# Gate logits by linearity in a pre-LN attention and feed-forward kernel

## Chip, cores and metric

The kernel runs on one core of one Trainium2 chip. The metric is the device time of one execution in microseconds. Lower is better. Times are told as the median of several runs; the profile is one further execution.

## What is computed

Two batches of 2048 tokens with 1024 features pass through two layers, all in float32. The first is attention with a head size of 256, the second a feed-forward layer with a router. Both take a normalised input and add their output to the residual.

```
x = x + attn(layernorm(x), Wqkv, bqkv, Wo, bo)      # q, k, v of width 256; softmax; @ Wo + bo
x = x + ffn(layernorm(x), ...)

def ffn(hidden, gate_w, up_w, down_w, fc1_w, fc2_w, expert_w, ln_gamma, ln_beta):
    logits = einsum('bsh,he->bse', hidden, gate_w)          # 8 experts
    routing_weights, _ = top_k(logits, 2)
    h = relu(einsum('bsh,hi->bsi', hidden, up_w)) ** 2      # 2048 wide
    shared_out = einsum('bsi,ih->bsh', h, down_w)
    x_latent = einsum('bsh,hl->bsl', hidden, fc1_w)         # 512 wide
    expert_out = einsum('bsl,lm->bsm', x_latent, expert_w)
    moe_out = expert_out * sum(routing_weights, axis=-1)
    routed_out = einsum('bsl,lh->bsh', moe_out, fc2_w)
    return layernorm(shared_out + routed_out, ln_gamma, ln_beta)
```

Of the router only one number per token is used: the sum of its two largest gate logits. It scales the latent part.

## The kernel before

Products keep nearly float32 accuracy by splitting each operand into a high part and a low part (`split`: ScalarE writes the high part, VectorE or GpSimd subtracts it for the low part). `Pass3` (L131) then issues three products for each pair of operands: high with high, low with high, high with low. Tokens are handled in eight blocks of 512 (`W`), each of four tiles of 128.

The kernel has four stages in order of time.

1. *Start* (`begin`). Expert weights are folded into fc2, the first block is normalised, and the QKV weights are split. The weights of V are stored with high and low parts side by side, 512 columns per chunk.
2. *QKV* (`a_block`, `qkv_block`). For each of eight blocks, V is computed in four tiles (`v_tile`, L447), then q and k in four chunks. Beside it, after each of the eight parts, the function `after(j)` normalises the next block, transposes it through DRAM and splits it. `NormBlock`, `Moments` and `Stats` hold the statistics. This stage, except for its last block, is written in the order in which it is issued (`manual_schedule`).
3. *Attention*. A loop over n computes the scores of block n, the values of block n - 1, and then `finish` and `project` (L726) for it: the product with Wo in two halves of 512 columns, multiplied by the inverse of the softmax sum and added to the residual, which already holds bo. The result goes to DRAM as `x1`. A scheduler orders the instructions here. The bank pools for TensorE's results are `psa` (four banks), `psb` and `psc` (two each).
4. *Feed-forward*. Four passes over two blocks each. An up stage and a down stage use a seven-product scheme on 2x2 block matrices (pieces `p1` to `p7`). Its order is written by hand. `next_piece` brings one weight piece: SP's queue loads it, ScalarE (L939) and VectorE (L946) split it. `Norm` normalises the blocks that come next, `Out` finishes the blocks that came before.

The gate sits in the up stages. `gate_part` (L995) multiplies one half of the normalised input with the gate weights: four products with 32 columns (8 high, 8 low, 16 zero) and four with 8 columns, all streaming 512 tokens. It is called four times in each up stage, for pieces p1, p2, p4 and p3; a copy on ScalarE (L1310) and three operations on VectorE (L1313, L1316, L1318) put the halves together. `Gate.largest` (L1013 to L1025) transposes the logits in 32x32 blocks, adds the high and low parts, takes the eight largest of each token (`max`, sixteen times), adds the first two, and transposes again. `send` (L1030) writes the result to DRAM and `spread` (L1034) reads it back to all partitions as `rwb`. Both are on POOL's queue. In the products that use them, the latent columns are multiplied by `rwb`.

`half` tiles (512 columns, four buffers), `row` tiles (1024 columns, nine) and `unit` tiles (2048 columns, fourteen) share the on-chip memory. Queues issue in order: SP's carries weights, residual rows and stores of `x1`; POOL's carries normalised tiles, kept weight pieces, bo, beta and the output.

Of the kernel before, what the change touches and what calls it, by code (L numbers as in the profile page):

```python
# [25 lines left out]
def kernel(  # L26
# [65 lines left out]

    def bank(pool, name):
        return pool.tile([P, W], FP, tag="b", name=name)
# [11 lines left out]
    bv_sb = half("bv")[:, :D]  # L106

    gate = const.tile([P, NCC, SQ], FR, name="gate")
    nc.vector.memset(gate.bitcast(FP), 0.0)
# [6 lines left out]
    fc2e = dram.tile([LAT, C], FP, name="fc2e")  # L116

# [54 lines left out]
    def ln_stats(parts, st=None):  # L172


        if st is None:
            st = small.tile([P, C // W, 6], FP, tag="st", name="st")
        for h, part in enumerate(parts):
            if part is not None:
                nc.vector.bn_stats(st[:, h, :], part)  # L179
        mv = small.tile([P, 2], FP, tag="mv", name="mv")  # L180
        nc.vector.bn_aggr(mv, st.rearrange("p a b -> p (a b)"))
        sd = small.tile([P, 1], FP, tag="sd", name="sd")
        nc.scalar.activation(sd, mv[:, 1:2], AF.Sqrt, bias=eps)
        return mv[:, 0:1], sd
# [11 lines left out]
    def norm_row(r, q=nc.gpsimd):  # L196
        return norm_write(r, row_stats(r), q)

    def row_stats(r):
        return ln_stats([r[:, ts(h, W)] for h in range(C // W)])  # L200

    def normalise(r, stats):
        mean, sd = stats
        nc.vector.tensor_scalar(r, r, mean, inverse(sd), ALU.subtract, ALU.mult)

    def norm_write(r, stats, q=nc.gpsimd):


        normalise(r, stats)
        return transpose_write(r, q)  # L210
# [44 lines left out]
    class Moments:  # L255


        def __init__(self, v, kind):
            self.v, self.kind = v, kind
# [5 lines left out]
        def new(self, a):  # L265
            return small.tile([P, 1], FP, tag=self.kind + a, name=a)
# [15 lines left out]
        def normalise(self):  # L282

            rs, nb = self.inverse(), self.new("nb")
            nc.vector.tensor_tensor(nb, self.nm, rs, ALU.mult)
            nc.scalar.activation(self.v, self.v, AF.Identity, scale=rs, bias=nb)  # L286

    class Stats(Moments):


        def __init__(self, v):
            self.v, self.kind = v, "n"
            mean, self.sd = row_stats(v)
# [6 lines left out]
    class NormBlock:  # L300
# [5 lines left out]
        def step(self, t):  # L306
            rows, m = self.rows, self.m
            if t == 0:
                m += [Moments(rows[0], "n"), Stats(rows[1])]
                m[0].second()  # L310
                m[0].normalise()
                m.append(Moments(rows[2], "n"))
# [4 lines left out]
            if t < NB:  # L317
                self.d.append(transpose_write(rows[t]))
                if t == 0:
                    m.append(Stats(rows[3]))  # L320
# [106 lines left out]
    def qkv_block(n, wqkv, xT, parts, after):  # L427
# [9 lines left out]
        def v_tile(t):  # L437
# [4 lines left out]
            for c in range(NCC):  # L442
                xh, xl = x_chunk(xT, c, ts(t, P))
                w = wqkv[2][c // 4].rearrange("p (c n) -> p c n", n=2 * D)[:, c % 4]
                ops = [(pm, xh, w), (pm[:, :D], xl, w[:, :D])]
                for i, (o, x_, w_) in enumerate(ops[:: -1 if c % 2 else 1]):
                    nc.tensor.matmul(  # L447
                        o,
# [3 lines left out]
                        stop=c == NCC - 1 and i == 1,  # L452
# [4 lines left out]
            nc.vector.tensor_tensor(vt, pm[:, D : 2 * D], vt, ALU.add)  # L457
# [29 lines left out]

    order = list(range(BPB, NBLK)) + list(range(BPB))
    def begin(wqkv, xT):
# [18 lines left out]
        nc.gpsimd.dma_start(out=bv_sb, in_=bqkv[2 * D : 3 * D].partition_broadcast(P))  # L508

# [52 lines left out]
        stats = [row_stats(first[0])]  # L562
        for t in range(NB):
            if t + 1 < NB:
                stats.append(row_stats(first[t + 1]))
            normalise(first[t], stats[t])
            if t == 1:
                r = [folded(0, accs)]
        wqkv[2] = []

        def beside(t, lc):
# [5 lines left out]
            if t in (1, 2):  # L577
                u = unit(f"w2_{t}")
                uv = u.rearrange("p (c n) -> p c n", n=2 * D)
                wv = ws[2][1].rearrange("p (c n) -> p c n", n=D)[:, ts(t - 1, NCC // 2)]  # L580
                split(wv, uv[:, :, 0:D], uv[:, :, D : 2 * D], nc.gpsimd)
                wqkv[2].append(u)
# [4 lines left out]
        return NormBlock(rows), r  # L587
# [120 lines left out]
    def project(n):  # L708
        s = st.pop(n)
        o = hl(s["oT"])  # L710
        for t in range(NB):
# [5 lines left out]
            for h in range(C // W):  # L717

                pm = bank(psa if n + 1 < NBLK else psc, "pw")
                acc = Pass3(pm, NDC)  # L720
                for dc in range(NDC):
                    acc.add(
                        tuple(o[:, i, ds(dc * W + t * P, P)] for i in range(2)),
                        piece(wo, dc, C, ts(h, W)),
                    )
                nc.vector.scalar_tensor_tensor(  # L726
                    r[:, ts(h, W)], pm, s["ri"][:, t : t + 1], r[:, ts(h, W)], ALU.mult, ALU.add
                )
            nc.sync.dma_start(out=x1[n][ts(t, P), :], in_=r)
# [4 lines left out]
    def a_block(i, norm, xT, x3):  # L734
# [5 lines left out]
        def after(j):  # L740
            if i + 1 == NBLK:
                if j == 0:
                    x3()
                elif j == 2 * NB - 1:
# [22 lines left out]
        qkv_block(order[i], wqkv, xT, V + QK, after)  # L767
        if nxt:
            return (after_next or [None])[0], nxt[0], lambda: split_tile(norm.x[3], 3, nxt[0])

    wqkv, xT = {}, new_xT("a")
    with tc.manual_schedule():
        steps = list(range(len(STEPS)))
        norm, fold = begin(wqkv, xT)
        x3 = lambda: None
        for i in range(NBLK - 1):
            norm, xT, x3 = a_block(i, norm, xT, x3)
# [9 lines left out]
    with tc.issue_after(fetched[0].ins):  # L787
        q_rows = [load_row(q_d[i], nc.gpsimd) for i in range(2)]
    a_block(NBLK - 1, None, xT, x3)

    with tc.issue_after(fetched[0].ins):
        wo_f = [load_row(Wo[ts(dc, P), :], nc.gpsimd) for dc in range(NDC)]

    g_f = half("g_f")[:, : NCC * NE].rearrange("p (c e) -> p c e", c=NCC)
    nc.gpsimd.dma_start(out=g_f, in_=gate_w.rearrange("(c p) e -> p c e", p=P))
    xts = []
    for n in range(1, NBLK + 1):
# [4 lines left out]
        for k in range(NKC + lag):  # L802
# [21 lines left out]
            elif k == 5 and n in range(3, 3 + NB):  # L824
                xts[n - 3] = norm_row(xts[n - 3], nc.sync)
# [8 lines left out]
            if n == 1 and k == NKC // 2:  # L834
                wo = unit("wo_h"), unit("wo_l")
                for dc in range(NDC):
                    split(wo_f[dc], *(v[:, ts(dc, C)] for v in wo))
                split(g_f, gate[:, :, 0:NE], gate[:, :, NE : 2 * NE])
# [151 lines left out]
    def gate_part(X, half):  # L990
        pg = bank(psc, "pg")
        for i in range(2):
            for c in range(4):
                m = NE if i else SQ
                nc.tensor.matmul(  # L995
                    pg[:m, :],
                    lhsT=gate[:, half * 4 + c, 0:m],
                    rhs=piece(X, c, W, slice(0, W))[i],
                    start=(i == 0 and c == 0),
                    stop=(i == 1 and c == 3),  # L1000
                )
        return pg[:SQ, :]

    class Gate:


        def __init__(self, gs):
            self.gs = gs

        def largest(self):  # L1010
            nb = W // SQ
            g, o = half("gtt")[:SQ, :], half("gtop")[:SQ, :]
            nc.vector.transpose(g, self.gs)  # L1013
            lg, m8 = (
                o[:, ds(i * nb * NE, nb * NE)].rearrange("p (b e) -> p b e", e=NE)
                for i in range(2)
            )
            gv = g.rearrange("p (b f) -> p b f", f=SQ)[:, :, 0 : 2 * NE]
            nc.vector.tensor_reduce(
                lg, gv.rearrange("p b (j e) -> p b e j", e=NE), AX.X, ALU.add  # L1020
            )
            for b in range(nb):
                nc.vector.max(m8[:, b, :], lg[:, b, :])
            nc.vector.tensor_tensor(o[:, 0:nb], m8[:, :, 0], m8[:, :, 1], ALU.add)
            nc.vector.transpose(o[:, ds(SQ, SQ)], o[:, 0:SQ])  # L1025
            self.rw = o[0:nb, ds(SQ, SQ)]

        def send(self):
            self.d = dram.tile([W // SQ, SQ], FP, tag="rw", name="rw_d", bufs=2)
            nc.gpsimd.dma_start(out=self.d, in_=self.rw)  # L1030

        def spread(self):
            rwb = half("rwb")
            nc.gpsimd.dma_start(  # L1034
                out=rwb, in_=self.d.rearrange("b i -> (b i)").partition_broadcast(P)
            )
            return rwb

    class Norm:
# [8 lines left out]
        def step(self, halves=(0, 1)):  # L1048
# [4 lines left out]
            if 0 in halves:  # L1053
# [4 lines left out]
                if norm in range(NB):  # L1058
                    self.m[norm].normalise()
            if 1 in halves:  # L1060
# [6 lines left out]
                if fetch in range(NB):  # L1067
                    self.x[fetch] = fetch_tile(self.d[fetch])
                self.i += 1
# [88 lines left out]
    with tc.manual_schedule():  # L1158
        for b in range(NBB):
# [72 lines left out]
            gm, gl = (6, 2) if b else (11, 1)  # L1232
            for m, (p, i) in enumerate(UPS[b]):
# [74 lines left out]
                if (p, i) == ("p1", 0 if b else 4):  # L1308
                    ga = half("ga")[:SQ, :]
                    nc.scalar.copy(ga, gate_part(X["p1"], 0))  # L1310
                elif (p, i) == ("p2", 0):
                    gs = half("gs")[:SQ, :]
                    add(gs, ga, gate_part(X["p2"], 1), ALU.add)  # L1313
                    gt = Gate(gs)
                elif (p, i) == ("p4", 1):
                    add(ga, ga, gate_part(X["p4"], 1), ALU.add)  # L1316
                elif (p, i) == ("p3", 6):
                    add(ga, ga, gate_part(X["p7"], 0), ALU.subtract)  # L1318
                    gt = Gate(ga)
                if m == gm or (p, i) == ("p3", 7):  # L1320
                    gt.largest()
                elif m == gm + gl or (p, i) == ("p3", 9):
                    gt.send()
# [150 lines left out]
```

## Time and profile before

| What | us |
|---|---|
| timed runs: median | 2317.57 |
| timed runs: lowest, highest | 2316.97, 2319.35 |
| profiled execution: its own time | 2321.8 |
| profiled execution: span on the core | 2320.0 |
| start, until V of the first block | 0 to 35 |
| eight QKV blocks | 35 to 302 |
| attention | 302 to 757 |
| four up stages | 757 to 952, 1143 to 1343, 1533 to 1731, 1922 to 2120 |
| four down stages | the stretches behind them, to 2320 |

The profile lists instructions by engine: PE is TensorE's products, PEld its weight loads, DVE is VectorE, ACT ScalarE, POOL GpSimd, SP the queue of SyncE. A line such as `pw<-wo_h,o` names what is written and what is read, and L131 is a line of the kernel. A product's length in the profile includes its way through the array, so the spacing of starts tells its cost in a row of products, not its length. The stage limits in the table are read from the first product of each kind in the timeline.

### The profile page before, as it was taken

How to read it: one execution, taken by the hardware profiler on the slowest of the kernel's cores; microseconds unless marked ns; L12 is line 12 of the kernel's file. 1: busy time of each engine (PE TensorE's matmuls, PEld its weight loads, DVE VectorE, ACT ScalarE, POOL GpSimd, SP SyncE). 2: the span in 40 equal slices, each digit the busy share in tenths (PEclk: the TensorE clock that was granted, in tenths of full speed). 3: DMA queues.
4: the chain of work that ended last, by engine and by line, in shares of the span. 5: the costliest groups of instructions: out<-in, count | busy, mean ns of one | idle time of the engine just before them, and what ended most of it. 6: DMA issues, size and time to landing. Idle time of an engine off the chain costs nothing.

```text
span 2320.0 us, 28848 instructions
## 1 busy us (share of the span) xinstructions
PE 2302.3 (99%) x10332; PEld 1894.8 (82%) x10332; DVE 1569.6 (68%) x2463; ACT 1187.1 (51%) x1955; POOL 284.3 (12%) x429
## 2 busy tenths in 40 slices
PE   9999999999999999999999999999999999999998
PEld 7888788888888788888878888888888888888886
DVE  6666569888878576797665577764456677435667
ACT  6555455555544633766562474664055566214245
POOL 3222211011000111110111111110000011000000
PEclk9999999999999999999999999999999999999999
DMA  7877749799986677786787688687568569556674
GB/s 255 296 279 278 245 140 263 229 303 295 228 192 188 216 225 227 258 286 199 216 240 246 228 306 313 186 250 218 192 217 273 192 210 274 188 186 198 204 223 150
DMA packets 236304, 540.28 MB, mean 233 GB/s; under 512 B 18513, under 2 KB 105041, under 8 KB 234113
## 3 DMA queue, kind: packets, MB, share of 16 engines
q1 hardware_dynamic: 170448, 301.25, 39.5%
q0 software_dynamic: 65712, 237.19, 35.0%
q8 instruction: 82, 1.34, 0.2%
q14 instruction: 62, 0.50, 0.1%
HBM read 411.47 MB, written 177.75 MB: 254 GB/s over the span
## 4 chain that ended last, share of the span: by engine, by line
PE 87%; DVE 6%; DMA 2%; issue 2%; ACT 2%; POOL 0%; SPq 0%; DVEq 0%; ACTq 0%; POOLq 0%
PE pd L131 33%; PE pu L131 31%; PE ps L131 8%; PE po L131 8%; PE pw L131 4%; DVE xblk L214 2%; PE pg L995 1%; DMA xt_d<-xblk 1%; DVE xla L144 1%; PE pq L131 1%; PE pf L131 1%; DVE st L179 1%; DMA raw<-in_L_ffn_up_w_dram 0%; ACT junk L274 0%; DVE v L457 0%
## 5 line engine op out<-in xcount | busy, mean ns | idle before, releaser
L131 PE MATMUL pd<-w,sp 128*128 128x512 f32 x3336 | 757.7, 390 | 0.1
L131 PEld LDWEIGHTS pd<-w,sp 128*128 128x128 f32 x3336 | 626.4, 188 | 130.3 <-DVE sp L1207 0.8
L131 PE MATMUL pu<-xh,w 128*128 128x512 f32 x2240 | 691.5, 390 | 1.9 <-DVE w L946 1.8
L131 PEld LDWEIGHTS pu<-xh,w 128*128 128x128 f32 x2240 | 420.7, 188 | 91.6 <-DVE w L946 2.7
L131 PE MATMUL pu<-xl,w 128*128 128x512 f32 x1120 | 436.6, 390 | 0.0
L131 PEld LDWEIGHTS pu<-xl,w 128*128 128x128 f32 x1120 | 210.4, 188 | 44.2 <-DVE xl L151 0.3
L1202 ACT CAST sp<-h 128x512 fp32r<-128x512 f32 x238 | 146.6, 618 | 155.7 <-PE pd L131 114.8
L939 ACT CAST w<-w 128x512 fp32r<-128x512 f32 x251 | 153.3, 616 | 131.1 <-DMA w<-wt 108.8
L946 DVE TENSOR_TENSOR w<-w 128x512 fp32r<-128x512 f32 x251 | 171.5, 685 | 69.4 <-ACT w L939 65.4
L1207 DVE TENSOR_TENSOR sp<-h,sp 128x512 fp32r<-128x512 f32 x238 | 162.8, 686 | 61.6 <-ACT sp L1202 61.5
L131 PE MATMUL po<-p,v 128*128 128x512 f32 x768 | 194.2, 391 | 0.0
L131 PE MATMUL ps<-q,k 128*128 128x512 f32 x768 | 192.6, 391 | 0.0
L131 PEld LDWEIGHTS ps<-q,k 128*128 128x128 f32 x768 | 143.8, 188 | 29.8 <-ACT max L630 0.2
L131 PEld LDWEIGHTS po<-p,v 128*128 128x128 f32 x768 | 143.3, 188 | 29.2
L1148 ACT ACTIVATE h<-h 128x1024 f32<-128x1024 f32 x48 | 50.8, 1059 | 219.7 <-DVE h L1265 163.2
L627 ACT COPY s<-ps 128x512 f32<-128x512 f32 x128 | 74.8, 585 | 142.4 <-PE ps L131 142.1
L151 DVE TENSOR_TENSOR xl<-xt,xh 128x512 fp32r<-128x512 f32 x108 | 74.3, 688 | 104.4 <-ACT xh L150 103.9
L214 DVE STREAM_TRANSPOSE xblk<-xrow 128x1024 f32<-128x1024 f32 x60 | 120.8, 2014 | 9.4 <-ACT xrow L286 9.2
L632 DVE TENSOR_TENSOR max<-ps,max 128x512 f32<-128x512 f32 x120 | 82.2, 685 | 33.7 <-ACT s L627 32.6
L131 PE MATMUL pq<-xha,w_h 128*128 128x512 f32 x256 | 99.9, 390 | 0.2 <-DVE v L457 0.2
L131 PE MATMUL pq<-xla,w_h 128*128 128x512 f32 x256 | 99.7, 390 | 0.0
L131 PE MATMUL pq<-xha,w_l 128*128 128x512 f32 x256 | 99.7, 389 | 0.0
(201 smaller groups left out, 2955.6 us busy)
## 6 DMA issues: line engine op xcount, KB each, us to landing
w<-w_p SPq DMA_DIRECT2D x225, 512.0 KB, 3.4
w<-wt SPq DMA_DIRECT2D x240, 256.0 KB, 3.3
w_p<-w POOLq DMA_DIRECT2D x90, 512.0 KB, 4.3
xt_d<-xblk POOLq DMA_DIRECT2D x56, 512.0 KB, 4.2
xt<-xt_d POOLq DMA_DIRECT2D x56, 512.0 KB, 6.0
xres<-in_L_attn_x_dram SPq DMA_DIRECT2D x32, 512.0 KB, 6.9
xres<-in_L_attn_bo_dram POOLq DMA_DIRECT2D x32, 512.0 KB, 10.5
x<-xres SPq DMA_DIRECT2D x32, 512.0 KB, 4.2
```

The source lines that it names most:

```text
L131: nc.tensor.matmul(self.ps, lhsT=a, rhs=b, start=self.i == 0, stop=self.i == self.n - 1, skip_group_check=self.on,)
L144: eng.tensor_tensor(lo, t, f32(hi), ALU.subtract)
L151: late_ops.append(lambda: nc.vector.tensor_tensor(lo, t, f32(hi), ALU.subtract))
L179: nc.vector.bn_stats(st[:, h, :], part)
L214: nc.vector.transpose(b.rearrange("p (q k i) -> p q k i", q=P // SQ, i=SQ), r.rearrange("p (k i q) -> p q k i", k=NCC, i=SQ),)
L627: nc.scalar.copy(s["s"][k // 4][:, ts(k % 4, W)], pm)
L632: nc.vector.tensor_tensor(s["max"], pm, s["max"], ALU.max)
L939: nc.scalar.copy(w[:, 0:W], raw)
L946: nc.vector.tensor_tensor(w[:, W : 2 * W], raw, f32(w)[:, 0:W], ALU.subtract)
L1148: nc.scalar.activation(o, v, AF.Relu)
L1202: nc.scalar.copy(t[:, 0:W], v)
L1207: add(t[:, W : 2 * W], v, f32(t)[:, 0:W], ALU.subtract)
```

## The change

The logits are linear in the normalised row, and the row is x1 = x + a Wo / s + bo, with s the softmax sum and a the attention's unnormalised output. So with G the gate weights and x1 having mean m and deviation d, the logits of a token are (x G + (a (Wo G)) / s + bo G - m (sum of G's rows)) / d. The largest two are chosen before the division by d, which keeps their order, and the sum is multiplied by 1/d. The parts come from four places:

- *x's part.* G stands as 8 high and 8 low columns behind V's weights. V's product gives x_normalised G in 16 columns. V's weights are stored anew: per chunk, 256 high columns and 16 gate columns in one piece (272), and 256 low columns apart. A chunk is now three products of 272, 256 and 264 columns in place of one of 512 and one of 256. The sums, with minus the mean and the deviation of x, go to DRAM (`xg_d`) by SP's queue, once per block. `gate_x` reads all of them at the start of attention and makes x G + bo G on VectorE in `logits`, which before held V's bias.
- *Attention's part.* Wo G (256 x 8) is made in the last QKV block by `gate_step`: 16 transposes of Wo, 16 products with 8 columns. It stands behind Wo's 1024 columns, 1032 in all, now as three pieces of 388, 388 and 256 columns in place of two of 512. `project` adds the last eight to `logits`.
- *Mean and deviation.* `Factor.tile` does three small operations on VectorE for each normalised tile; `send` writes the result to DRAM. The column sums of G and bo G come from one product with ones.
- *Loads.* The gate weights are loaded twice, once at the start. Wo's rows, the gate weights and bo are loaded on POOL's queue ahead of the two q rows that begin attention.

`gate_part` and `Gate` are gone, with the copy and the three operations that joined the halves; `spread` stays, and reads what `Factor` sent. The core of the diff:

```diff
+    logits = const.tile([P, NBLK * NB * NE], FP, name="logits")
+    bv_sb = logits[:, :D]
+    g_sum = const.tile([P, 3, NE], FP, name="g_sum")
...
+    class Factor:
+        def __init__(self, n):
+            self.n, self.f = n, per_token()
+        def tile(self, t, mean, g, rs):
+            v, m8 = (self.f[:, i, 0:NE] for i in range(2))
+            lg = logits[:, ds((self.n * NB + t) * NE, NE)]
+            nc.vector.scalar_tensor_tensor(v, g_sum[:, g], mean, lg, ALU.mult, ALU.add)
+            nc.vector.max(m8, v)
+            nc.vector.scalar_tensor_tensor(
+                self.f[:, t, NE : NE + 1], m8[:, 0:1], m8[:, 1:2], rs, ALU.add, ALU.mult
+            )
+        def send(self, q):
+            q.dma_start(out=rw_d[self.n].rearrange("t p -> p t"), in_=self.f[:, :, NE])
...
             for c in range(NCC):
                 xh, xl = x_chunk(xT, c, ts(t, P))
-                w = wqkv[2][c // 4].rearrange("p (c n) -> p c n", n=2 * D)[:, c % 4]
-                ops = [(pm, xh, w), (pm[:, :D], xl, w[:, :D])]
-                for i, (o, x_, w_) in enumerate(ops[:: -1 if c % 2 else 1]):
+                wh, wl = v_weights(wqkv[2], c)
+                ops = [(xh, wh), (xh, wl), (xl, wh[:, : D + NE])]
+                for i, (x_, w_) in enumerate(ops):
                     nc.tensor.matmul(
...
             nc.vector.tensor_tensor(vt, pm[:, :D], bv_sb, ALU.add)
-            nc.vector.tensor_tensor(vt, pm[:, D : 2 * D], vt, ALU.add)
+            nc.vector.tensor_reduce(
+                xg[:, t, 0:NE],
+                pm[:, D : D + 2 * NE].rearrange("p (j e) -> p e j", e=NE),
+                AX.X,
+                ALU.add,
+            )
+            if t == NB - 1:
+                xg_n = xg_d[:, ts(n, NB * (NE + 2))].rearrange("p (t e) -> p t e", e=NE + 2)
+                nc.sync.dma_start(out=xg_n, in_=xg)
...
-                split(wv, uv[:, :, 0:D], uv[:, :, D : 2 * D], nc.gpsimd)
+                nc.scalar.copy(uh[:, :, 0:D], wv)
+                sub(ul, wv[:, 0:3], uf[:, 0:3, 0:D], ALU.subtract)
+                sub(r[:, ts(t - 1, D)], wv[:, 3], uf[:, 3, 0:D], ALU.subtract)
+                g = g_f[:, ts(t - 1, NCC // 2)]
+                split(g, uh[:, :, D : D + NE], uh[:, :, D + NE : DG], nc.gpsimd)
...
-            for h in range(C // W):
-                pm = bank(psa if n + 1 < NBLK else psc, "pw")
+            for h in range(3):
+                pm = bank(psa if n + 1 < NBLK else psc, "pw")[:, : WO[h]]
...
-                nc.vector.scalar_tensor_tensor(
-                    r[:, ts(h, W)], pm, s["ri"][:, t : t + 1], r[:, ts(h, W)], ALU.mult, ALU.add
-                )
+                lg = logits[:, ds((n * NB + t) * NE, NE)]
+                rt = r[:, ds(h * WO[0], min(WO[h], C - h * WO[0]))]
+                for o_, a in ((rt, pm[:, : rt.shape[-1]]), (lg, pm[:, WO[2] - NE : WO[2]])):
+                    if h == 2 or o_ is rt:
+                        nc.vector.scalar_tensor_tensor(
+                            o_, a, s["ri"][:, t : t + 1], o_, ALU.mult, ALU.add
+                        )
+    WO = (388, 388, 256)
...
+    def gate_step(j):
+        if j < 4:
+            if j % 2 == 0:
+                wo_t.append(row("wo_t"))
+            pt = bank(psc, "pt")
+            pv = pt.rearrange("p (c d n) -> p c d n", d=NDC, n=P)
+            for c in range(2):
+                for dc in range(NDC):
+                    nc.tensor.transpose(pv[:, c, dc], wo_f[dc][:, ts(2 * j + c, P)], ident)
+            nc.scalar.copy(wo_t[-1][:, ts(j % 2, W)], pt)
+            return
...
+        nc.tensor.matmul(
+            pt[:, : 2 * NCC * NE], lhsT=ones.to_broadcast([P, P]), rhs=g_h[:, : 2 * NCC * NE],
+            start=True, stop=True,
+        )
...
+        for dc in range(NDC):
+            pt = bank(psc, "pt")
+            for c in range(NCC):
+                nc.tensor.matmul(
+                    pt[:, 0:NE],
+                    lhsT=wo_t[c // 4][:, ds((c % 4) * NDC * P + dc * P, P)],
+                    rhs=g_f[:, c],
...
+    def gate_x():
+        h = half("xg")[:, : NBLK * NB * (NE + 2)]
+        nc.sync.dma_start(out=h, in_=xg_d)
...
+        tt(lv, y, over(h[:, :, NE + 1 : NE + 2], 1), ALU.mult)
+        tt(y, over(g_sum[:, 2], 0), over(h[:, :, NE : NE + 1], 1), ALU.mult)
+        tt(lv, lv, y, ALU.add)
+        tt(lv, lv, over(g_sum[:, 1], 0), ALU.add)
...
+                elif 2 <= j < 2 * NB - 1:
+                    gate_step(j - 2)
...
-                if (p, i) == ("p1", 0 if b else 4):
-                    ga = half("ga")[:SQ, :]
-                    nc.scalar.copy(ga, gate_part(X["p1"], 0))
-                elif (p, i) == ("p2", 0):
-                    gs = half("gs")[:SQ, :]
-                    add(gs, ga, gate_part(X["p2"], 1), ALU.add)
-                    gt = Gate(gs)
-                elif (p, i) == ("p4", 1):
-                    add(ga, ga, gate_part(X["p4"], 1), ALU.add)
-                elif (p, i) == ("p3", 6):
-                    add(ga, ga, gate_part(X["p7"], 0), ALU.subtract)
-                    gt = Gate(ga)
-                if m == gm or (p, i) == ("p3", 7):
-                    gt.largest()
-                elif m == gm + gl or (p, i) == ("p3", 9):
-                    gt.send()
-                elif m == gm + gl + 2 or (p, i) == ("p7", 1):
-                    rwb[p == "p7"] = gt.spread()
+                if m == gm:
+                    rwb[0] = spread(2 * b)
+                elif (p, i) == ("p7", 1):
+                    rwb[1] = spread(2 * b + 1)
```

## The prediction

> **What bounds the kernel now.** I read the page's busy times and the shares of its chain of waits first, then the windows, then the timelines around the lines that the change touches.
>
> ```profile
> PE 2302.3 (99%) x10332; PEld 1894.8 (82%) x10332; DVE 1569.6 (68%) x2463; ACT 1187.1 (51%) x1955; POOL 284.3 (12%) x429
> ...
> PE 87%; DVE 6%; DMA 2%; issue 2%; ACT 2%; POOL 0%; SPq 0%; DVEq 0%; ACTq 0%; POOLq 0%
> ```
>
> TensorE is busy 99% of the span and holds 87% of the chain that ended last. So the sum is made on TensorE's row of instructions: a product that goes gives back its spacing to the next one, and another engine counts only where it makes TensorE wait. The windows tell where that can happen (columns: window, its length, then busy us of PE, PEld, DVE, ACT and POOL, the clock, the DMA share and GB/s):
>
> ```profile
> 427.00:483.00 56.00, 56.00 (x256) 46.15 (x255) 48.71 (x58) 29.68 (x40) 7.10 (x8) 1.00 0.79 242
> 1143.00:1183.00 40.00, 40.00 (x177) 31.63 (x176) 26.72 (x52) 27.68 (x56) 7.97 (x12) 1.00 0.97 275
> 1183.00:1188.00 5.00, 3.23 (x14) 2.37 (x13) 2.59 (x5) 4.93 (x10) 0.00 (x0) 1.00 0.34 129
> ```
>
> One attention block keeps VectorE busy 48.71 of 56 us. The start of the second up stage keeps the DMA engines 97% busy, and behind it TensorE loses 5.00 - 3.23 = 1.8 us to a late weight piece.
>
> **The products removed.** The timeline of TensorE shows one gate product between two up products (start, length, line, how many):
>
> ```profile
> 1145.26 0.39 PE L131 MATMUL pu<-xl,w 128*128 128x512 f32 x1
> 1145.49 1.07 PE L995 MATMUL pg<-xh,gate 128*32 128x512 f32 x4
> 1146.40 1.09 PE L995 MATMUL pg<-xl,gate 128*8 128x512 f32 x4
> 1147.33 0.62 PE L131 MATMUL pu<-xh,w 128*128 128x512 f32 x2
> ```
>
> The up product before it starts 0.23 us ahead, as everywhere; the eight gate products hold TensorE from 1145.49 to 1147.33, 1.84 us. Four such groups in each of four up stages: 16 x 1.84 = 29.4 us removed, all on the engine that sets the end.
>
> **V's wider columns.** Before, a chunk is one product of 512 columns and one of 256:
>
> ```profile
> 70.08 0.63 PE L447 MATMUL pv<-w,xha 128*128 128x512 f32 x2
> 70.54 0.39 PE L447 MATMUL pv<-w,xla 128*128 128x256 f32 x2
> 70.77 0.62 PE L447 MATMUL pv<-w,xha 128*128 128x512 f32 x2
> ```
>
> Two of each take 0.69 to 0.70 us: 0.23 for one of 512, 0.115 for one of 256, 0.35 for a chunk. After, a chunk is 272, 256 and 264 columns. With (0.227 - 0.115) / 256 = 0.00044 us a column that is 0.122 + 0.115 + 0.119 = 0.356, 0.006 more. 8 blocks x 4 tiles x 8 chunks = 256 chunks: +1.4 us. From below 0.8; from above 3.5, if three narrow products in a row cost 0.005 us more each (before has only two in a row). Its eviction gets shorter: a 256-wide add of 424 ns becomes a sum over 16 columns (a 32x256 sum at L1019 took 418 ns, a 128x4 reciprocal 179), so VectorE has cover.
>
> The dispute here is the weight load. Every product has its own, 188 ns in the row of PEld, longer than the 115 ns between two 256-wide products; yet these start 115 ns apart, so loads overlap products. The Trainium skill (TensorE: Matmul & The Clock Gate, section "The mechanism") says that a weight load overlaps a running matmul "only when row_grp differs", which speaks against this change: all products here use all 128 rows. With its 128 / 1.2 = 107 ns for 128 columns (same page, section "LDWEIGHTS (loading the stationary operand)"), the 256 + 192 added products would cost an estimated 448 x 0.107 = 48 us, and the time would rise by some 29 us; by the row above it falls by the 18.9 of the sum below. I take the row.
>
> **Wo's columns.** A token tile's 12 products of 512 columns (0.227 each, 2.72 us) become 12 of 388 (0.173) and 6 of 256 (0.115): 2.77. 32 tiles x 0.042 = +1.3 us (0.8 to 2.5). Their eviction on VectorE, 0.66 us from start to start for 512 columns, becomes twice 0.53, 0.39 and some 0.13 for the eight logits: 1.58 for 1.32 before, 1.04 more for the four tiles of a block. The timeline of VectorE shows what room it has in that stretch:
>
> ```profile
> 487.27 0.75 DVE L726 SCALAR_TENSOR_TENSOR xres<-pw,ri,xres 128x512 f32<-128x512 f32 x1 [0.63 <-PE pw L131]
> ...
> 492.48 0.75 DVE L726 SCALAR_TENSOR_TENSOR xres<-pw,ri,xres 128x512 f32<-128x512 f32 x1 [0.18 <-PE pw L131]
> ...
> 495.20 0.75 DVE L726 SCALAR_TENSOR_TENSOR xres<-pw,ri,xres 128x512 f32<-128x512 f32 x1 [0.17 <-PE pw L131]
> ```
>
> It waits 0.63 + 0.18 + 0.17 = 0.98 us for TensorE there. The first bank now ends 0.3 us sooner, so the 1.04 fits nearly; VectorE ends about 0.3 us later, as TensorE does itself (4 x 0.042 and pipeline). Four banks let TensorE run ahead. Behind the evictions the running maximum (L632) is queued, which frees score banks. I put +0.5 us for all blocks (0 to 4). The four element-wise operations over 256 columns that make x's logits (some 1.5 us) and the three tiny ones per normalised tile (about 0.45) lie in first blocks and norm steps where VectorE has gaps; uncovered, 1.5 + 32 x 0.45 = 16 us, but only if TensorE waited for each.
>
> **The new products in the last QKV block.** 16 transposes (before: eight from 24.48 to 25.27, 0.099 each): 1.6 us. 16 full-precision products of 8 columns: the nearest row is the sum of exponentials, where each shows as two records:
>
> ```profile
> 425.50 0.95 PE L702 MATMUL psum<-ones,sum 128*128 128x1 f32 x8
> 426.30 0.96 PE L131 MATMUL ps<-q,k 128*128 128x512 f32 x3
> ```
>
> Four products in 0.80 us, 0.2 each: 3.2. The column sums (128 columns) lie between 0.2 and four transposes, 0.4: 0.3. Together +5.1 (4.6 to 6). Wo's two rows, the gate weights and bo now go ahead of the two q rows on POOL's queue, 0.5 to 0.9 us to issue each. In before the first two loads behind q's store were issued at 267.94 and 268.48 and took 6.4 and 7.9 us; in their place Wo lands by about 276.4. The first transposes come after V's third tile, 268.3 + 3 x 2.8 = 276.8 at the earliest. Close: +0.3 (0 to 2), and V's fourth tile is queued behind. The q rows land some 3 us later than before, near 280, and are needed near 297. The eight stores of x's gate columns on SP stand ahead only of loads for attention, needed from 330 on.
>
> **The start.** TensorE waits for expert weights until 10.40 while the queues are full. One more load, the gate weights, joins: its packets took 0.5 us of each DMA engine in before. +0.4 (0 to 0.5). V's low parts on POOL are now 768, 256 and 64 elements: about 0.5 us more behind the 2.38 us of before, with V at 35.3 and the second ready at 33.2: hidden; uncovered it is 0.5.
>
> **The up stages without the gate.** Here lies the largest doubt: weights are staged by ACT, VectorE and DMA, and TensorE arrives 3.7 us earlier at every piece behind the two early groups. But VectorE's queue stood still for the gate's sum:
>
> ```profile
> 1148.65 0.69 DVE L946 TENSOR_TENSOR w<-raw,w 128x512 fp32r<-128x512 f32 x1 [1.22 <-ACT w L939]
> 1154.84 0.68 DVE L1313 TENSOR_TENSOR gs<-ga,pg 32x512 f32<-32x512 f32 x1 [5.50 <-PE pg L995]
> 1155.45 0.67 DVE L946 TENSOR_TENSOR w<-w 128x512 fp32r<-128x512 f32 x1
> ```
>
> 5.5 us, with the weight split behind it, whose end lets the next raw load go. The DMA view of 1143 to 1183 has one hole of some 3 us, just after this. If the wait goes, the hole closes, and the transfers move up by about as much as TensorE does. So the 1.8 us stall neither goes nor grows by the whole 3.7: +1.0 (-1.9 to +3.7). In the first up stage the piece split at 789.38 to 790.63 was in use at 790.3 to 793.1: no slack, VectorE full; the wait of 3.09 us before 774.25 goes, four times 0.45 us of logits come in: +0.5 (0 to 1.5).
>
> **Sum.** -29.4 + 1.4 + 1.3 + 0.5 + 5.1 + 0.3 + 0.4 + 1.0 + 0.5 = -18.9 us. Span 2320.0 - 18.9 = 2301.1. The profiled execution took 2321.8, 1.8 around its span, and 4.2 more than the median 2317.57 of the timed runs; the difference is taken off the median: 2298.7. All lower bounds together give -25.1 (2292.5), all upper ones -5.7 (2311.9).
>
> **The rivals.**
> *Transfers bound the up stages.* For: the 97%, and the stall behind it. Against: the hole. If three of the four stages give back 3.7 us each in place of the 1.0: -18.9 - 1.0 + 11.1 = -8.8, 2308.8. Chance 0.14.
> *VectorE bounds attention.* For: 48.71 of 56 us. Against: the room shown. If the 1.04 us of each of eight blocks is paid in full, with 0.45 for four tiles: +10.1 in place of 0.5, 2308.3. Chance 0.1. With both, 2318: no change. Chance 0.03.
> *Weight loads set the pace of narrow products* (ends slower). If a load of 188 ns can't be started before the last one ends, V's chunk takes 3 x 0.188 = 0.564, +0.214 x 256 = 55 us, and a Wo tile 18 x 0.188 = 3.38, +0.66 x 32 = 21: 2298.7 - 2.7 + 76 = 2372. It decides from about 0.073 us a chunk on (18.9 / 256), that is at 0.143 a narrow product in place of 0.119. For: three in a row were never run. Against: 0.115 twice in a row, and 0.099 for transposes. Chance 0.06.
>
> **How the numbers follow.** My forecast has 0.67. Faster (under 2312.9, 0.2% being about what a measurement can tell) are the forecast and the two single rivals: 0.91; no change 0.03; slower 0.06. The range reaches from all lower bounds to the single rivals with a little beyond: 2291.5 to 2310. The forecast's own is 2293 to 2305.
>
> **What would show it.** No gate product between 1143 and 1155; V's chunk at 0.356 us and Wo's tile at 2.77 in the timeline; 5 us of transposes and small products before attention; the stall near 1180 at 1 to 4 us. It is wrong if V's chunk exceeds 0.43, if TensorE shows waits for VectorE's maximum in every attention block, or if stalls for weight pieces appear in all up stages.

## The result and the profile after

| | median, us | lowest to highest | ratio to before, 95% interval |
|---|---|---|---|
| before | 2317.93 | 2316.36 to 2320.48 | |
| changed | 2323.88 | 2317.50 to 2331.49 | 1.0026 (1.0017 to 1.0034) |

The change made the kernel 6 us slower, where 18.9 us of gain were forecast. Its runs also spread over 14 us, those of before over 4. The profiled execution of the changed kernel took 2328.16 us, 2326.3 of it span. The page's busy times and its chain of waits by engine:

```profile
PE 2297.2 (99%) x10702; PEld 1923.4 (83%) x10702; DVE 1559.2 (67%) x2466; ACT 1188.4 (51%) x1960; POOL 287.6 (12%) x434
...
PE 87%; DVE 5%; DMA 5%; issue 2%; ACT 1%; SPq 0%; POOL 0%; DVEq 0%; ACTq 0%; POOLq 0%
```

TensorE works 5 us less (2302.3 before), yet the span is 6.3 us longer, and DMA's share of the chain has gone from 2% to 5%. Something waits for transfers that did not before. The place is found by stages, each from its first TensorE product to that of the next; the first up stage is counted from the end of the last projection, as some up products stand ahead of it. The last two columns are two of the experiments below: the first has no sends, the second is the best version.

| Stage, us | before | changed | no_send | rows_send4 |
|---|---|---|---|---|
| start and QKV | 301.8 | 312.1 | 310.3 | 309.6 |
| attention | 454.9 | 462.0 | 462.0 | 460.8 |
| first up, down | 195.5, 190.5 | 197.1, 193.9 | 189.5, 191.0 | 190.6, 190.9 |
| second up, down | 200.0, 190.4 | 190.5, 193.4 | 190.5, 190.4 | 190.4, 190.4 |
| third up, down | 197.9, 190.4 | 193.5, 190.6 | 193.4, 190.4 | 192.3, 190.4 |
| fourth up, down | 197.9, 200.7 | 192.9, 200.6 | 191.2, 200.7 | 190.4, 200.9 |

Up to the feed-forward part the changed kernel loses 17.3 us, where 9.0 were forecast. In the feed-forward part it gains only 11.1, where 27.9 were forecast. The first up stage got longer where it should have got shorter by some 7 us, and so did the first two down stages, of which no term of the forecast spoke.

The timeline of TensorE in the changed kernel, in the first up stage:

```profile
821.34 0.39 PE L135 MATMUL pu<-xl,w 128*128 128x512 f32 x1
824.37 0.78 PE L135 MATMUL pu<-xh,w 128*128 128x512 f32 x1 [2.64 <-ACT w L1091]
827.79 0.80 PE L135 MATMUL pu<-xh,w 128*128 128x512 f32 x1 [2.65 <-DVE w L1098]
828.38 0.63 PE L135 MATMUL pu<-xl,w 128*128 128x512 f32 x1
828.81 1.05 PE L135 MATMUL pu<-xh,w 128*128 128x512 f32 x2
```

Two products start 3.03 and 3.42 us after the one before, in place of 0.23, because a weight piece is not split yet; the next ones start 0.43 us apart, with a granted clock of 0.50 from 827 to 831. The timeline of ScalarE, which splits first, names what it waits for:

```profile
823.70 0.62 ACT L1091 CAST w<-raw 128x512 fp32r<-128x512 f32 x1 [9.50 <-DMA raw<-in_L_ffn_fc_w_dram]
```

ScalarE sat idle for 9.5 us until the raw weights landed. The DMA view of two windows of the changed kernel shows what is slow (columns: what is written and read, queue, how many, size of each, median us from issue to landing). First 780 to 800:

```profile
raw<-in_L_ffn_up_w_dram SPq DMA_DIRECT2D x4, 256.0 KB, 2.7
...
raw<-in_L_ffn_fc_w_dram SPq DMA_DIRECT2D x2, 256.0 KB, 2.9
```

Then 806 to 822:

```profile
w<-wt SPq DMA_DIRECT2D x4, 256.0 KB, 11.3
raw<-in_L_ffn_fc_w_dram SPq DMA_DIRECT2D x2, 256.0 KB, 14.3
...
rwb<-rw POOLq DMA_DIRECT2D x1, 256.0 KB, 12.2
rw<-xg POOLq DMA_DIRECT2D x1, 2.0 KB, 12.8
```

A weight piece of 256 KB that lands in 2.7 us takes 11 to 14, and so does a transfer of 2 KB issued among them: `rw<-xg` is `Factor.send`. Part of this is the crowd of other transfers in that stretch. In no_send, the version without sends, the same loads (804 to 820) take

```profile
w<-wt SPq DMA_DIRECT2D x4, 256.0 KB, 6.1
raw<-in_L_ffn_fc_w_dram SPq DMA_DIRECT2D x2, 256.0 KB, 8.6
```

So what comes with the send is 5 to 6 us. Its source `f[:, :, NE]` has one number every 40 bytes, its target is turned round (`t p -> p t`), so it consists of 512 separate elements of 4 bytes. The send before this change wrote 16 rows of 128 bytes. The DMA view of before has it as

```profile
rw_d<-gtop POOLq DMA_DIRECT2D x8, 2.0 KB, 5.0
```

### The profile page after: what moved, and what is told of

It reads as the page before. It is cut to its first block, busy times and chain, and to the rows that moved or that the text cites. A ratio compares the mean times of both kernels' runs of the same rounds, so it can differ in the third digit from the quotient of the medians.

```text
span 2326.3 us, 29644 instructions
## 1 busy us (share of the span) xinstructions
PE 2297.2 (99%) x10702; PEld 1923.4 (83%) x10702; DVE 1559.2 (67%) x2466; ACT 1188.4 (51%) x1960; POOL 287.6 (12%) x434
## 4 chain that ended last, share of the span: by engine, by line
PE 87%; DVE 5%; DMA 5%; issue 2%; ACT 1%; SPq 0%; POOL 0%; DVEq 0%; ACTq 0%; POOLq 0%
PE pd L135 29%; PE pu L135 28%; PE pq L135 8%; PE ps L135 7%; PE po L135 6%; PE pv L472 4%; PE pw L135 4%; DMA w<-wt 3%; DMA raw<-in_L_ffn_up_w_dram 1%; DVE w L1098 1%; DVE xblk L234 1%; DMA xrow<-in_L_attn_x_dram 0%; PE pf L135 0%; DVE s L722 0%; DVE sp L1320 0%
## 5 line engine op out<-in xcount | busy, mean ns | idle before, releaser
L135 PE MATMUL ps<-q,k 128*128 128x512 f32 x768 | 192.9, 391 | 0.0
```

Source lines behind the costliest of these rows:

```text
L135: nc.tensor.matmul(self.ps, lhsT=a, rhs=b, start=self.i == 0, stop=self.i == self.n - 1, skip_group_check=self.on,)
```

## The experiments

Theory S says that the sends, by their many tiny elements, hold up the weight pieces. Theory D says that the transfers are simply too many for a TensorE that arrives earlier. Theory C concerns the clock in the last QKV block, theory F the price of narrow products, theory V the start of attention.

**The sends left out (no_send).**

```diff
         def send(self, q):
-            q.dma_start(out=rw_d[self.n].rearrange("t p -> p t"), in_=self.f[:, :, NE])
+            pass
...
-        nc.gpsimd.dma_start(out=rwb, in_=rw_d[n].rearrange("t p -> (t p)").partition_broadcast(P))
+        nc.gpsimd.dma_start(out=rwb, in_=gate_w[0 : W // NE].rearrange("t p -> (t p)").partition_broadcast(P))
```

> The eight sends of the routing factors are left out, and the spread reads 512 of the gate weights in their place, so the latent part is scaled by other numbers. Theory S (a send writes 512 separate elements of 4 bytes; it takes 12 to 14 us to land, and weight pieces in flight beside it land late): the stalls of TensorE near 821 to 831, 1056, 1130, 1437 and 1515 us go, 10 to 15 us in all, and the time falls from 2323.9 to 2309 to 2314. Theory D (the transfers are simply too many for a TensorE that arrives earlier): the sends are 2 KB each and don't matter; 2322 to 2326, with the stalls where they are or a little later.

Measured: 2313.67 us (before, on the same chip: 2318.47; ratio 0.9982, 0.9973 to 0.9991), 10.2 less than the changed kernel. The window from 795 to 832, of the changed kernel and then of this one (columns: window, length, busy us of PE, PEld, DVE, ACT and POOL, granted clock, DMA share, GB/s):

```profile
795.00:832.00 37.00, 31.46 (x128) 24.87 (x127) 17.43 (x29) 22.66 (x39) 6.03 (x10) 0.91 0.76 194
```

```profile
795.00:832.00 37.00, 36.73 (x162) 30.03 (x161) 21.43 (x37) 23.20 (x38) 6.29 (x10) 1.00 0.78 242
```

With the DMA engines as busy (0.76 and 0.78), they move 194 or 242 GB/s, TensorE is idle 5.5 or 0.3 us of 37, and its granted clock is 0.91 or 1.00. The stalls near 821, 1056, 1130, 1437 and 1515 us are all gone, and the first three down stages are back at 190.4 to 191.0. DMA's share of the chain is back at 2%:

```profile
PE 90%; DVE 4%; issue 2%; DMA 2%; ACT 2%; POOL 0%; SPq 0%; DVEq 0%; POOLq 0%; ACTq 0%
```

That is theory S. Theory D fits what is left: 0.97, 0.50 and 1.22 us near 1570 in the third up stage, 0.62 in the fourth.

**The same sends in the kernel before (before_sends).**

```diff
+    def extra_send(n, q):
+        q.dma_start(out=dump[n].rearrange("t p -> p t"), in_=dsrc[:, :, NE])
...
+                if fetch == NB - 1:
+                    extra_send(self.n, nc.gpsimd)
...
+            elif k == 5 and n == 3 + NB:
+                extra_send(0, nc.sync)
```

> The kernel before with eight sends of 512 elements of 4 bytes added at the places where the changed kernel has them, and nothing else. Theory S: stalls appear in the first up stage, the first down stage and the second down stage as in the changed kernel, and the time rises by 8 to 14 us, to 2326 to 2332. Theory D: eight transfers of 2 KB change nothing, 2317 to 2319.

Measured: 2329.70 us, ratio 1.0046 (1.0033 to 1.0058), 11.2 more than before. Each kernel pays 10 to 11 us for its sends. Nothing waits for these ones, so it is their being in flight that costs; through which part of the DMA path they hold up the loads is not shown. Seven stand near the places of the changed kernel's. The eighth, meant for attention, went out at 21.1 us already, and start and QKV did not get longer by it (299.9 us). The profiled execution was the shortest of its five, span 2323.1, and shows stalls of 0.3 to 1.4 us near 811, 1037, 1113, 1501 and 1891. The first up and the first down stage are 1.9 and 3.0 us longer than before, the second down stage only 0.6.

**Is it the elements or the scattered writes (sends_packed)?** before_sends with `dump` as `[P, NB]` and `out=dump[n]`: the writes lie side by side, the reads do not.

> before_sends with the added sends written as 16 bytes next to each other for each partition; they are still read as 512 separate elements of 4 bytes. If the number of elements sets the time, a send takes 12 to 14 us as in before_sends. If scattered writes of 4 bytes to DRAM set it, it takes 6 to 8 us, as in send16.

The DMA views of before_sends and of this kernel:

```profile
dump<-dsrc POOLq DMA_DIRECT2D x7, 2.0 KB, 12.8
```

```profile
dump<-dsrc POOLq DMA_DIRECT2D x7, 2.0 KB, 14.5
```

The one execution took 2340.38 us. Packing the writes alone does not help, so the scattered writes are not what makes a send slow. That fits the number of elements; strided reads alone would fit as well, and reads that lie side by side with scattered writes were not run. The Trainium skill (DMA: Bandwidth & Descriptors, section "Rules for kernel authors") says that a last dimension that is strided or not contiguous becomes one descriptor per element, and should be rearranged to be contiguous. The runs agree as far as they go: 512 elements took 12.6 us and 128, in the next experiment, 7.1; the descriptors themselves do not show in the traces.

**Fewer elements (send16).** The four factors of a partition are kept side by side, and the products read them with a stride.

```diff
+            self.rw = small.tile([P, NB], FP, tag="rw", name="rw", bufs=2)
...
-            q.dma_start(out=rw_d[self.n].rearrange("t p -> p t"), in_=self.f[:, :, NE])
+            q.dma_start(out=rw_d[self.n], in_=self.rw)
...
+        return rwb.rearrange("p (i t) -> p t i", t=NB)
```

> Nothing is left out: the four factors of a partition stand side by side and are sent as 128 elements of 16 bytes in place of 512 of 4 bytes; the products with the factors read them with a stride. Theory S: the send takes a fourth of the time, 3 to 5 us, and the stalls shrink to a fourth or less; 2310 to 2316. If each send cost a fixed latency and its number of elements did not matter: as after, 2322 to 2326. Theory D: 2322 to 2326.

The DMA view of the changed kernel, then of send16:

```profile
rw<-xg POOLq DMA_DIRECT2D x7, 2.0 KB, 12.6
```

```profile
rw<-rw POOLq DMA_DIRECT2D x7, 2.0 KB, 7.1
```

2314.95 us, ratio 0.9985 (0.9976 to 0.9994). A fourth of the elements gives back 8.9 of the 10.2 us, although a send still takes 7.1 us, more than the 3 to 5 expected. What is left behind a send are 0.6 us near 821, 1.5 near 972 and 0.4 near 1354.

**The small products (send16_beside).** The timeline of the changed kernel in the last QKV block:

```profile
299.61 0.38 PE L831 MATMUL pt<-g_f,ones 128*128 128x128 f32 x2
299.83 4.69 PE L845 MATMUL pt<-g_f,wo_t 128*128 128x8 f32 x32
304.37 0.77 PE L135 MATMUL pq<-xha,w_h 128*128 128x512 f32 x1
304.94 0.63 PE L135 MATMUL pq<-xha,w_l 128*128 128x512 f32 x1
305.37 0.63 PE L135 MATMUL pq<-xla,w_h 128*128 128x512 f32 x1
```

The small products take 4.5 us, and then products of 512 columns start 0.43 us apart, ten of them until 308.8. TensorE was never idle there. The windows show that its clock (the third number from the end) falls within the row of small products:

```profile
299.60:302.00 2.40, 2.40 (x24) 2.39 (x22) 0.58 (x4) 1.62 (x2) 0.00 (x0) 1.00 0.35 140
302.00:304.30 2.30, 2.30 (x14) 2.30 (x14) 0.61 (x1) 0.00 (x0) 0.00 (x0) 0.54 0.28 27
304.30:308.80 4.50, 4.50 (x12) 3.53 (x13) 1.30 (x2) 0.00 (x0) 0.00 (x0) 0.50 0.84 259
```

The edit puts the small products between the next chunk's:

```diff
                 acc.add(piece(wqkv[i], c, D, ts(dc, P)), x_chunk(xT, c))
+                if beside:
+                    beside[-1](c)
```

> send16, and the 16 small products of the last QKV block are put two at a time between the products of the chunk of k that follows, in place of in a row before it. Theory C (a row of small products lowers TensorE's clock, and ten products after it take 427 ns in place of 227): those ten go back to 227, 2.0 us less than send16. Rival: the slow products come from the scores that begin there, and the order of the small ones doesn't matter: within 0.5 us of send16.

The timeline of send16_beside:

```profile
301.34 0.51 PE L851 MATMUL pt<-g_f,wo_t 128*128 128x8 f32 x4
301.70 0.47 PE L135 MATMUL pq<-xha,w_h 128*128 128x512 f32 x1
302.01 0.39 PE L135 MATMUL pq<-xha,w_l 128*128 128x512 f32 x1
302.24 0.40 PE L135 MATMUL pq<-xla,w_h 128*128 128x512 f32 x1
```

No product of 512 columns takes 0.43 us any more, and the clock stays at 1.00:

```profile
299.00:308.50 9.50, 9.50 (x60) 8.38 (x59) 2.44 (x5) 1.75 (x3) 0.00 (x0) 1.00 0.49 157
```

The scores start at 308.5 in place of 310.5 in send16: theory C, with 1.9 of its 2.0 us, though in send16's own trace it is seven products that start 0.43 us apart, not ten. 2313.81 us, ratio 0.9978 (0.9968 to 0.9988); of the 1.9 the medians show 1.1, less than their intervals can tell.

**Narrow products alone (before_v3).** The kernel before, with V's chunk as three products of 256 columns.

```diff
-                ops = [(pm, xh, w), (pm[:, :D], xl, w[:, :D])]
+                ops = [(xh, w[:, :D]), (xh, w[:, D : 2 * D]), (xl, w[:, :D])]
```

> The kernel before with V's chunk as three products of 256 columns in place of 512 and 256, all into the same 256 columns, and one addition of the eviction less. Theory F (each product costs a fixed 12 to 14 ns beside 0.417 ns a column): the three come at 0.118 us each, a chunk at 0.354 in place of 0.345, V's products take 2 to 3 us more in all. Rival (only the odd widths 272 and 264 are dear, or three in a row are): 0.115 each and 0.345 a chunk, no more than before; or 0.125 each.

Its timeline:

```profile
70.09 0.40 PE L447 MATMUL pv<-w,xha 128*128 128x256 f32 x2
70.33 0.28 PE L447 MATMUL pv<-w,xla 128*128 128x256 f32 x1
70.45 0.40 PE L447 MATMUL pv<-w,xha 128*128 128x256 f32 x2
```

0.36 us for three: 0.120 each, between theory F's 0.118 and the rival's 0.125. A row of narrow products pays about 0.005 us more a product than the 0.115 of two in a row. V's products took 92.1 us in all, 1.8 more than before. In before 0.9 us of waits stand among them, at 234 and 274, and none here; so the products themselves cost 2.7 more, within the 2 to 3 of theory F.

**No transfer at all (pe_spread).** send16_beside without sends and spreads: TensorE transposes a factor column that is repeated along the free side, which spreads it over all partitions.

```diff
+        rwb, pt = half("rwb"), bank(psc, "pr")
+        for t in range(NB):
+            nc.tensor.transpose(
+                pt[:, ts(t, P)], factors[n][:, t : t + 1].to_broadcast([P, P]), ident
+            )
+        nc.scalar.copy(rwb, pt)
```

> send16_beside without the sends and without the spreads: per block four TensorE transposes of a factor column, read with stride nothing along the free side, make the 128 x 512 factors in a bank, and ScalarE copies them out. Theory S and the full transfers: the stalls that are left behind a 16-byte send (1.5 us near 968, 0.4 near 1352) go, and the 256 KB of each spread leave the stretch in which raw weight pieces of the third and fourth up stages take 11 to 14 us to land, so their stalls (2.6 us near 1570) go or halve; 8 x 4 transposes at 0.1 cost 3.3 us. Together 2.5 us less to 1 us more than send16_beside: 2311 to 2315. If the transposes cost 0.2 each or lower the clock, 2316 or more.

2312.40 us, ratio 0.9968 (0.9958 to 0.9979), as expected. The 32 transposes start 0.109 us apart and cost about 3.5 us, so what the transfers no longer hold up is nearly spent. The stall near 1570 is absent, but one of 1.2 us is at 1190, and pe_spread_gp below, with no sends or spreads either, has 1.6 at 1573 again. Why it comes and goes is open.

**The spread later (late_spread).** send16_beside with `gm = 14` in every up stage.

> send16_beside with the first spread of the later three up stages four pieces (11 us) later, and nothing else. If the 256 KB of the spread are what makes the raw pieces late near 1570 us, that stall (2.6 us) shrinks to under 1 us, and the time falls by 1 to 2.5 us. If loads and stores of the blocks that are finished there are enough by themselves, the stall stays at 2 us or more, and the time is within 0.7 us of send16_beside (2313.8).

The stall near 1570 stayed (0.45, 0.50 and 1.35 us), so the spread is not what makes it: the first spread of that stage now goes out at 1574.2, when the first two of these waits are over, and the other transfers of that stretch suffice. The time, 2310.48 us (0.9963, 0.9949 to 0.9976), is better than the expectation that belongs to this; its interval meets that of send16_beside, and the profiled spans differ by 0.6 us only (2308.7 and 2309.3).

**Rows of 128 bytes, and gate_x on POOL (rows_send4).** late_spread with two edits:

```diff
+            o = half("rwt")[:, :SQ]
+            nc.vector.transpose(o, self.rw)
+            for a in range(P // SQ):
+                q.dma_start(out=rw_d[self.n][:, ts(a, SQ)], in_=o[ds(a * SQ, NB), :])
...
-        tt, y = nc.vector.tensor_tensor, h[:, :, 0:NE]
+        tt, y = nc.gpsimd.tensor_tensor, h[:, :, 0:NE]
```

> late_spread with two edits. VectorE transposes the factors in 32 x 32 blocks, so that a send is 16 rows of 128 bytes (four transfers of four rows) in place of 128 elements of 16 bytes; and the four operations of gate_x are on POOL in place of VectorE. Theory S: 16 elements land in 2 to 7 us and hold nothing up; the stalls of 1.5 us near 968 and 0.4 near 1351 go. Theory V (gate_x makes VectorE late in the first attention block): the waits of 0.2, 0.4 and 0.5 us at 349 to 362 go or halve. Together 1.5 to 3 us less than late_spread: 2307.5 to 2309.5. If four more issues on POOL's queue cost as much as they save: 2310 to 2312.

Its DMA view and its chain by engine:

```profile
rw<-rwt POOLq DMA_DIRECT2D x28, 0.5 KB, 4.3
```

```profile
PE 93%; DVE 3%; DMA 1%; issue 1%; ACT 1%; POOL 0%; SPq 0%; DVEq 0%; POOLq 0%; ACTq 0%
```

2308.45 us, ratio 0.9954 (0.9941 to 0.9968): 9.4 us faster than before and 15.4 faster than the changed kernel by the medians. Its interval meets that of late_spread, from which it differs by 2.0. DMA's share of the chain falls to 1%. The waits behind the sends near 968 and 1351 and those at 349 to 362 are gone. That such a send holds nothing up is not so everywhere: in the first up stage its transfers took 7 to 8 us, and a wait of 1.1 us at 819 is new. Of the waits near 1570 one of 1.8 us is left.

**gate_x alone (pe_spread_gp).** pe_spread with the same line changed.

> pe_spread with the four operations of gate_x on POOL in place of VectorE. Theory V: the waits at 348 to 362 us (0.2, 0.4, 0.5) go or halve: 0.5 to 1.1 less than pe_spread, 2311 to 2312. If the splits of Wo on VectorE make the first block late, nothing changes.

2309.67 us, ratio 0.9962 (0.9949 to 0.9974). The waits at 348 to 362 went: attention took 460.8 us in place of 462.0, a little more than theory V's 0.5 to 1.1. The medians fell by 2.7, of which 1.5 are those of the kernel before in the two comparisons (2319.40 and 2317.89).

## Why the prediction was wrong

| Step of the prediction | forecast, us | measured in the trace, us |
|---|---|---|
| gate products, up stages' stalls and logits, without sends | -27.9 | -26.4 (no_send) |
| the sends | not in the sum | +15.4 (traces); +10.2 (medians) |
| V's columns | +1.4 | +3.2 |
| Wo's columns | +1.3 | +3.5 |
| new products in the last QKV block | +5.1 | +6.2 |
| the clock behind them | not in the sum | +2.0 |
| VectorE in attention | +0.5 | +2.1 |
| Wo's loads late | +0.3 | 0 |
| start | +0.4 | +0.3 |

The two products' rows and VectorE's are differences of summed start-to-start times, VectorE's those of the products of scores and values. In return some 1.6 us of stalls that before had among the products of q and k are absent. The -26.4 and the 15.4 are differences of the feed-forward part: 1563.3 us before, 1536.9 without sends, 1552.3 with. Five up products (1.1 us) moved ahead of the last projection and count to attention, so like for like the first row is -25.3. Two waits in the first up stage are new in every version without the gate: in no_send 1.5 us near 783, for a split of the input, and 0.3 near 801, where the forecast had 0.5 in all.

*The step that failed* is "The up stages without the gate". It asked whether transfers would come too late, looked at how full the queues were, and counted four VectorE operations of 0.45 us; the send that goes with them was described in the change but had no price, and the down stages, where six of the sends lie, no term at all. The runs show 10.2 us in its place by the medians of the changed kernel and of no_send. By the traces the four sends of the first two down stages go with 3.4 and 3.0 us more there, the two of the third with 0.2. The row that would have warned was there: the send of before is also 2 KB, but in 16 rows of 128 bytes. The new form was visible in the one line of `send`. Its kind of harm was visible as well: the raw loads are 1.8 us late at 1183 already in before.

*The sends are not the whole miss.* The changed kernel took 25.2 us more than the 2298.7 forecast. Without the sends it takes 2313.7, still 15.0 more and above the range's 2310. Of these, 8.1 us stand in the profile: a span of 2309.2 for a forecast of 2301.1, most of it from terms that the table shows to be too small. The other 6.9 are chance in two profiles, as the last paragraph of this section tells.

*What the step said besides was right.* VectorE's wait of 5.50 us for the gate's sum went, and the hole in the transfers closed. This is the line of DMA shares in the view of 1165 to 1205 of the changed kernel, each digit the tenths of one us:

```profile
DMA  9999999999999589999979999999999999999802
```

No 0 stands before the last three digits. The line of before, for 1143 to 1183, has three low digits in the middle:

```profile
DMA  9999999999999910099999999999999998999999
```

The second up stage's stall went with it: 9.5 us gained there, at the good end of the range given. The rival that transfers bound the up stages came true in small: without sends, 2.7 us in the third up stage and 0.6 in the fourth, where 3.7 each in three stages were priced.

*Two terms were also mis-sized.* V's chunk is 0.125, 0.118 and 0.121 us, 0.364 in place of 0.356, and Wo's 388 columns take 0.178 in place of 0.173, its 256 take 0.118 in place of 0.115. Both lie above their bounds. Wo's 3.5 us are over its 2.5. V's +3.2 seem to lie within 3.5, but the V of before has 0.9 us of waits in it; by the products alone a chunk went from 0.349 us to 0.365 in the mean, 4.1 us in all. These waits and the 1.6 us among q and k are chance at least in part: before_sends, with the same QKV code, ends QKV 1.9 us earlier than before. The straight line between 512 and 256 columns was taken through a 256 that had a wide product near it; before_v3 shows 0.120 in a row. The rival of weight loads that set the pace was wrong, as argued: far from 0.143.

The Trainium skill (TensorE: Matmul & The Clock Gate, section "Back-to-back issue gap") gives N / 2.4 + 2.5 ns for N columns, and says itself that it counts too little at small N. For 256 and 388 columns that is an estimate of 109 and 164 ns; the 118 and 178 measured here decide.

*The small products* were priced from four among long ones, and took a little more than the upper bound (6.2 for 6). The clock makes this excess too: up to 302.1 us the records of the row start 0.112 us apart, the last ten 0.213, which is 1.0 us more in all. Without that they come to 5.1, the forecast. That a row of them lowers the clock for themselves and for what follows was in no row of the profile of before.

By the profiled executions no_send is 10.8 us faster than before, by the medians 4.8: the profiled execution of before was 4.2 us above the median beside it, that of no_send 2.6 below its own. Part of the gain that a sum on one execution shows is thus the luck of that execution. The two together are the 6.9 us.

## What to carry to other kernels

Look at the form of a transfer, not its size: 2 KB as 512 elements of 4 bytes took 12 to 14 us and made weight pieces of 256 KB on another queue 5 to 6 us later than without it. Put the numbers side by side before they are sent, which already gave back most of the loss here, or turn them round on VectorE. A saving on the engine that bounds the kernel is worth what the suppliers of the next pieces allow, so price each new transfer in every stage where it is in flight, also those that the change does not name. Where small products stand in a long row, try them between large ones.

## What was not expected of the hardware

- Between 512 elements of 4 bytes, 128 of 16 and rows of 128 bytes, a send took 12.6, 7.1 and 4.3 us. With the first kind in flight the DMA engines, counted as busy for 0.76 of a window of 37 us, moved 194 GB/s; without it 242 at 0.78.
- TensorE's granted clock fell without an idle stretch: some 2.4 us into a row of products with 8 columns it went from 1.00 to 0.50, and behind the row, of 4.5 us, ten products of 512 columns started 0.427 us apart in place of 0.227. Behind the two stalls of 3 us the same was seen for some six products, at a clock of 0.50. Put between large products, the same small ones left it at 1.00.
- A factor column read with stride nothing and transposed on TensorE is spread over all partitions at 0.109 us per 128 tokens.
